# The gated attention of a recurrent layer dealt out with the experts' work, its last block in a place of its own, and six row products moved from VectorE to GpSimd

## The chip, the cores and the metric

The kernel runs on one core of a Trainium2 chip. The metric is the device time of one execution in microseconds (us). Engines are written as in the profile: PE is TensorE (PEld its weight loads), DVE is VectorE, ACT is ScalarE, POOL is GpSimd, SP is SyncE, which here only issues DMAs. Each engine takes its instructions strictly in order, from a queue of its own.

## The reference

The input x has 8 sequences of 512 steps and 256 features; all is in 32 bits. Two branches read the same normalised rows, and their product is added to x:

```python
xn = layernorm(x)
# recurrent attention, 16 heads of 16, for each sequence and step:
S = S * exp(gk); S = S + k * (a @ S + v); o = q @ S
attn = layernorm(o * sigmoid(xn @ Wog1 @ Wog2)) @ Wo
# mixture of experts, the best 2 of 8 for each of the 4096 rows:
moe = layernorm(sum over the two of w_e * (gelu(xn @ W1[e] + b1[e]) @ W2[e] + b2[e]))
out = x + attn * silu(moe)
```

## The kernel before

The 512 steps are cut into 8 blocks of 64 (all 8 sequences together: 512 rows to a block), and a block into chunks of 16 or 8 steps, alternately by block, 48 chunks in all. The recurrence walks the chunks in order; its arithmetic within a chunk (`fine`, `solve`) is done on DVE ahead of the walk. A chunk of the walk is `by_state` (products with the state S on PE, L901, and the decayed copy of S on ACT, L911), `add_v` (DVE, L932, and the rows it stores to `ro`, L943 and L948), `by_keys` (PE, L966) and `renew` (DVE, L978). Two blocks later the block's output is made: `load_output` (R from `ro`, 16 to a half, L1009 and L1012) and `output` (DVE, L1029 and L1038, stored as `o`, L1042).

The experts' branch is a list of 39 tiles of up to 256 sorted rows (`experts`). A tile loads 1 MB for each of its two weights (`w`, L1069 and L1071, on SP, two places in turn), gathers rows (L1081, POOL), multiplies (`ph`, L1125), takes gelu (`h`, L1133), multiplies again (`py`, L1150), scales by the gate's weight (`y`, L1158) and scatters with addition into `y_dram` (L1102, POOL). It also copies x to out piece by piece (L1139, SP).

`attend(s)` is the rest of the attention branch for block s. It loads the state's part (`by_state`, L1196, 8 DMAs) and the block's own part (`o_f`, L1204, 2 DMAs), then the inner gate rows (`og`, L1210, 2 DMAs), all on SP; it adds (DVE, L1213), makes the outer gate (PE `p`, L1220, written "p2" in the code and the text; sigmoid `sg` on ACT, L1224), multiplies (DVE, L1227), normalises (`moments` on DVE, L1171 and L1172; `deviation`, with the square root on ACT at L1177 and L1179, L1180 on DVE; `normed` on ACT, L1184), transposes (`pz`, L1241; `zT`, L1242) and multiplies by Wo (`po`, L1248). For blocks 0 to 5 the result is copied (ACT, L1265) and stored to `att_d` (POOL, L1269). Blocks 6 and 7 (`LATE`) multiply the gated sums `g` by `po` straight out of PSUM (DVE, L1256) and store them into `out` with addition (POOL, L1259). The tiles o, t and og1 have one place each, and the next block's loads wait until the last reader is done.

After the experts, `fetch_sums` loads the eight blocks of sums (`g`, L1275, POOL), and `finish(s)` normalises them, applies gamma and beta (DVE, L1291 and L1293) and silu (ACT, L1294); for blocks 0 to 5 it loads the stored attention (`att_f`, three places, L1302, POOL), multiplies (DVE, L1304) and stores into `out` with addition (two DMAs, L1307, POOL).

The order around the change: three queues of generators. `inner` holds the work ahead of the walk and the outputs, `beside` the experts and later the `finish` of all blocks (four lanes), `between` the attention. `both(share, other)` spends `share` on `inner`, a share on `between` and `other` on `beside`, in eight rounds; a generator yields the cost of what it has issued, or WAIT. After the 48th chunk the three are spent at 3.0 each until they are empty. The order in which a framework's scheduler then hands the instructions to each engine follows these turns.

Of the kernel before, what the change touches and what calls it, by code (L numbers as in the profile page):

```python
# [9 lines left out]
F32 = mybir.dt.float32  # L10
I32 = mybir.dt.int32
AF = mybir.ActivationFunctionType
ALU = mybir.AluOpType
# [4 lines left out]
P = 128  # L18
NB = 64
# [11 lines left out]
def recurrent_attn_moe_kernel(  # L31
# [23 lines left out]
    nc = tc.nc  # L55
    B, T, D = x.shape
    H = Wgamma.shape[1]
    HD = D // H
    E, _, DFF = W1.shape
    KD = D // P  # L60
    NF = DFF // P
    NTB = T // NB
    NP = B * NB // P
# [15 lines left out]
    def bank(name):  # L79
        return ps_p.tile([P, 512], F32, tag="ps", name=name)  # L80
# [30 lines left out]
    kqd_d, g_d, og_d, f1_d, v_d, fq_d, pc_d, kt_d, ro_d, o_d, att_d = ([] for _ in range(11))  # L111
# [28 lines left out]
    sp = ctx.enter_context(tc.tile_pool(name="inner", bufs=2))  # L140
    vz = []
    for i in range(2):
        t = sp.tile([P, GC, 2 * D], F32, name=f"vz{i}", bufs=1)
# [9 lines left out]
    made, now = {}, {}  # L153
# [192 lines left out]
    for q in range(4):  # L346
        for n in range(4):
            lo = 32 * q + E * n
# [292 lines left out]
    def behind(ins, first):  # L641

        tc.add_manual_dep(
            ins.ins,
            first.ins.name,
            mybir.DependencyInfo(mybir.DependencyClass.NoSync, mybir.DependencyReason.DATA),
            reason="what it waits for has that long",
        )
# [199 lines left out]
    solved = []  # L848


    cp, pending = [], []
# [209 lines left out]
    LATE = (NTB - 2, NTB - 1)  # L1061
    WAIT = "nothing to do yet"
# [106 lines left out]
    def moments(pool, t, i, mv):  # L1169
        st = pool.tile([P, 6], F32, name="st_f", bufs=4)  # L1170
        nc.vector.bn_stats(st, t)  # L1171
        nc.vector.bn_aggr(mv[:, i], st)  # L1172
# [10 lines left out]
    def normed(t, i, r):  # L1183
        nc.scalar.activation(  # L1184
            t, t, AF.Identity, bias=r[:, 1, i : i + 1], scale=r[:, 0, i : i + 1]
        )

    def attend(s):
        while (s, NB // CS[s] // 2 if s == NTB - 1 else 0) not in loaded:
            yield WAIT  # L1190
        pool = cp[0]
        o = pool.tile([P, NP, D], F32, name="o_f", bufs=1)
        t = pool.tile([P, NP, D], F32, tag="t_f", name="by_state", bufs=1)
        for bb in range(2):
            for q in range(4):
                nc.sync.dma_start(  # L1196
                    t[bb * NB : (bb + 1) * NB, q],
                    ro_d[s][q, CS[s] :, :, bb * D : (bb + 1) * D].rearrange("i c d -> c i d"),
                )
            yield 1.0  # L1200
        while s not in written:
            yield WAIT
        for bb in range(2):
            nc.sync.dma_start(  # L1204
                o[bb * NB : (bb + 1) * NB],
                o_d[s].rearrange("t (c bb) d -> bb t c d", bb=2)[bb],
            )
        og1 = pool.tile([32 + HD, B * NB], F32, name="og1", bufs=1)
        for lo in (0, 32):
            nc.sync.dma_start(og1[lo : lo + HD], og_d[s])  # L1210
        for _ in range(1 if s in LATE else SLACK):
            yield 1.0
        behind(nc.vector.tensor_tensor(o, o, t, ALU.add), now["work"])  # L1213
        yield 1.2
        sg = pool.tile([P, NP, D], F32, tag="t_f", name="sg", bufs=1)
        p2s = [bank("p2").rearrange("p (n d) -> p n d", n=2) for _ in range(NP // 2)]
        for k in range(2):
            for i, p2 in enumerate(p2s):
                at, n = slice(32 * i, 32 * i + HD), 2 * i + k
                nc.tensor.matmul(  # L1220
                    p2[:, k], og1[at, n * P : (n + 1) * P], wog2_sb[at], start=True, stop=True
                )
        for i, p2 in enumerate(p2s):
            nc.scalar.activation(sg[:, 2 * i : 2 * i + 2], p2, AF.Sigmoid)  # L1224
        yield 1.0
        yield 1.0
        nc.vector.tensor_tensor(o, o, sg, ALU.mult)  # L1227
        mv = pool.tile([P, NP, 2], F32, name="mv_f", bufs=1)
        for i in range(NP):
            moments(pool, o[:, i], i, mv)  # L1230
        yield 3.0
        r = yield from deviation(pool, mv)
        for i in range(NP):
            normed(o[:, i], i, r)
        yield 1.0
        zT = pool.tile([P, NP, KD, P], F32, tag="t_f", name="zT", bufs=1)
        for i in range(0, NP, 2):
            pz = bank("pz").rearrange("p (n j t) -> p n j t", n=2, j=KD)
            for k in range(2):
                for j in range(KD):  # L1240
                    nc.tensor.transpose(pz[:, k, j], o[:, i + k, j * P : (j + 1) * P], ident)  # L1241
            nc.scalar.copy(zT[:, i : i + 2], pz)  # L1242
            yield 1.0
        for i in range(0, NP, 2):
            po = bank("po").rearrange("p (n d) -> p n d", n=2)
            for k in range(2):
                for j in range(KD):
                    nc.tensor.matmul(  # L1248
                        po[:, k], zT[:, i + k, j], wo_sb[:, j],
                        start=(j == 0), stop=(j == KD - 1),  # L1250
                    )
            if s in LATE:
                while s not in gated:
                    yield WAIT
                g = gated[s][:, i : i + 2]
                nc.vector.tensor_tensor(g, g, po, ALU.mult)  # L1256
                yield 2.0
                for bb in range(2):
                    nc.gpsimd.dma_start(  # L1259
                        rows_of(out, s, bb)[:, i : i + 2],  # L1260
                        g[bb * NB : (bb + 1) * NB],
                        accum_op=ALU.add,
                    )
                continue
            nc.scalar.copy(o[:, i : i + 2], po)  # L1265
            yield 2.0
        if s in LATE:
            return
        nc.gpsimd.dma_start(att_d[s].rearrange("n p d -> p n d"), o)  # L1269
        attended.append(s)  # L1270
# [10 lines left out]
    def finish(fp, s, g):  # L1281
        mv = fp.tile([P, NP, 2], F32, name="mv_g", bufs=4)
        for i in range(NP):
            moments(fp, g[:, i], i, mv)
        yield 2.5
        r = yield from deviation(fp, mv)
        for i in range(NP):
            normed(g[:, i], i, r)
        yield 1.0
        wide = [P, NP, D]  # L1290
        nc.vector.tensor_tensor(g, g, now["gam"].unsqueeze(1).to_broadcast(wide), ALU.mult)  # L1291
        yield 1.2
        nc.vector.tensor_tensor(g, g, now["bet"].unsqueeze(1).to_broadcast(wide), ALU.add)  # L1293
        nc.scalar.activation(g, g, AF.Silu)  # L1294
        yield 1.2
        if s in LATE:
            gated[s] = g
            return
        while s not in attended:
            yield WAIT  # L1300
        att = fp.tile([P, NP, D], F32, name="att_f", bufs=3)
        nc.gpsimd.dma_start(att, att_d[s].rearrange("n p d -> p n d"))  # L1302
        yield 1.0
        nc.vector.tensor_tensor(g, g, att, ALU.mult)  # L1304
        yield 1.2
        for bb in range(2):
            nc.gpsimd.dma_start(  # L1307
                rows_of(out, s, bb), g[bb * NB : (bb + 1) * NB], accum_op=ALU.add
            )
# [41 lines left out]
    def both(share, other):  # L1351
        for _ in range(8):
            inner.spend(share / 8)
            between.spend(share / 16)
            beside.spend(other / 8)

    late = ExitStack()
# [8 lines left out]
    def everything_else():  # L1366

        for s in range(2, NTB):
            yield from project(s, xT_all[:, s])
        while not cp:  # L1370
            yield WAIT
        projecting.close()
        prologue.close()
        with tc.tile_pool(name="moe", bufs=2, side="right") as mp:
            yield from experts(mp)
        fp = late.enter_context(tc.tile_pool(name="fin", bufs=2, side="right"))
        for name, ap in (("gam", gamma), ("bet", beta)):
            now[name] = fp.tile([P, D], F32, name=f"{name}_sb", bufs=1)
            nc.sync.dma_start(now[name], ap.partition_broadcast(P))
        sums = [fetch_sums(fp, s) for s in range(NTB)]  # L1380
        yield 1.0
        for s in range(NTB):
            beside.queue.append(finish(fp, s, sums[s]))

    inner, beside, between = Work(1), Work(4), Work(1)
    beside.queue += [sorting(), everything_else()]

    def with_output(s):
# [8 lines left out]
        )  # L1397

    def attention():
        for s in range(NTB):  # L1400
            yield from attend(s)

    def recurrence():
# [59 lines left out]
    fetch(0)  # L1463
    turn_keys(0)
    inner.queue.append(recurrence())
    between.queue.append(attention())
    cost = fine_cost(0)
    for _ in range(4):
        both(cost / 4, EARLY / 4)
# [8 lines left out]
    n = NB // CS[NTB - 1]  # L1478
# [39 lines left out]
```

## Time and profile before

| | us |
|---|---|
| median of 3 runs | 1146.72 |
| lowest and highest | 1145.83, 1148.68 |
| the profiled execution's own time | 1136.74 |
| its span in the trace | 1135.0 |
| PE, DVE, ACT, POOL busy | 884.4, 882.3, 657.4, 372.7 |
| mean granted TensorE clock | 0.875 |
| by-state products of chunk 48 begin | 986.6 |
| last scaling of an expert's rows (L1158) begins | 1056.8 |
| first moments of the sums (L1171) begin | 1070.4 |
| last store into out is issued | 1129.7 |

Times within the profile count from the start of its span. A line number is one of the kernel before. A group of instructions is read as line, engine, operation, output<-inputs, shape, count, then busy time and mean of one, then the engine's idle time just before them and what ended it.

### The profile page before, as it was taken

The page shows a single profiled execution, that of the slowest core. Times are in us where ns is not written, and L with a number is a line of the kernel's source. Part 1 is how long each engine was busy: PE and PEld are TensorE (multiplying, and loading weights), DVE is VectorE, ACT ScalarE, POOL GpSimd, SP SyncE. Part 2 cuts the span into 40 slices and gives each one's busy share as a digit, 9 for nine tenths or more (in the row PEclk, how much of TensorE's full clock was granted, in tenths as well). Part 3 has the DMA queues.
Part 4 walks back from the last instruction along what each step waited for, and adds up shares of the span by engine and source line. Part 5 has one row for each costly group of instructions (what it writes and reads, how often), then busy time and mean ns, then how long its engine had stood idle before and what let it go on. Part 6 is the DMA issues. An engine that isn't in the chain of part 4 may idle for free. (4 is left out here: it accounts for less than half of the span.)

```text
span 1135.0 us, 24853 instructions
## 1 busy us (share of the span) xinstructions
PE 884.4 (78%) x9448; PEld 685.0 (60%) x9448; DVE 882.3 (78%) x1769; ACT 657.4 (58%) x1559; POOL 372.7 (33%) x312
## 2 busy tenths in 40 slices
PE   4979988636889989797969976989799599867402
PEld 2534645325777778576858754877677488756301
DVE  6479998957999998699999679999698183321494
ACT  2664537447455759745695665556955446535485
POOL 3300000052237633245324331367433243320334
PEclk9986998758899999889989996999899799887756
DMA  9666688598577999969789896878969979983786
GB/s 224 181 175 193 157 229 147 125 272 247 122 200 228 126 262 238 190 194 217 221 172 204 191 252 157 212 248 229 143 190 252 157 193 221 209 218 104 225 189 106
DMA packets 393254, 221.86 MB, mean 195 GB/s; under 512 B 280912, under 2 KB 362704, under 8 KB 392112
## 3 DMA queue, kind: packets, MB, share of 16 engines
q1 hardware_dynamic: 363248, 172.17, 61.4%
q0 software_dynamic: 25280, 43.93, 18.4%
q10 hardware_dynamic: 4608, 4.20, 1.5%
q8 instruction: 74, 1.21, 0.5%
q14 instruction: 44, 0.36, 0.1%
HBM read 152.07 MB, written 72.35 MB: 198 GB/s over the span
## 5 line engine op out<-in xcount | busy, mean ns | idle before, releaser
L1125 PE MATMUL ph<-xT_s,w 128*128 128x256 f32 (+1 forms) x1248 | 289.1, 389 | 13.8 <-DMA w<-in_L_ffn_W_dram 7.2
L1150 PE MATMUL py<-w,h 128*128 128x256 f32 x1136 | 270.0, 394 | 22.4 <-ACT h L1133 18.1
L1125 PEld LDWEIGHTS ph<-xT_s,w 128*128 128x128 f32 x1248 | 235.0, 207 | 50.4 <-issue 9.7
L1102 POOL DMA_INDIRECT y_dram<-y,target x71 | 159.3, 2244 | 316.9 <-ACT y L1158 154.2
L1150 PEld LDWEIGHTS py<-w,h 128*128 128x128 f32 x1136 | 218.5, 197 | 56.3 <-ACT h L1133 20.7
L911 ACT ACTIVATE sdec<-S,PcF 128x64 f32<-128x64 f32 x752 | 189.4, 341 | 91.4 <-DVE S L978 87.8
L1133 ACT ACTIVATE h<-ph,bias 128x256 f32<-128x256 f32 (+1 forms) x312 | 121.7, 453 | 97.8 <-PE ph L1125 97.5
L1081 POOL DMA_INDIRECT xs<-xn_dram,source x71 | 113.8, 1602 | 138.8 <-PE pt L1094 111.7
L978 DVE SCALAR_TENSOR_TENSOR S<-PC,heads,sdec 128x256 f32<-128x256 f32 x188 | 78.8, 473 | 51.9 <-PE PC L966 47.5
L1158 ACT ACTIVATE y<-py,weight 128x256 f32<-128x256 f32 x71 | 33.3, 469 | 87.5 <-PE py L1150 87.4
L901 PE MATMUL PC<-S,FA 64*16 64x64 f32 (+1 forms) x3072 | 44.3, 232 | 43.2 <-DVE S L978 43.0
L966 PE MATMUL PC<-RO,KT 8*64 8x64 f32 (+1 forms) x3008 | 49.4, 246 | 34.4 <-DVE RO L932 24.7
L966 PEld LDWEIGHTS PC<-RO,KT 8*64 8x64 f32 (+1 forms) x3008 | 41.5, 143 | 53.9 <-DVE RO L932 31.5
L811 DVE TENSOR_TENSOR scratch_a<-Z,A 128x1020 f32<-128x1020 f32 (+21 forms) x88 | 66.5, 756 | 5.3 <-ACT fq L775 4.7
L901 PEld LDWEIGHTS PC<-S,FA 64*16 64x16 f32 (+1 forms) x3072 | 34.7, 100 | 59.5 <-DVE S L978 49.9
L736 DVE TENSOR_TENSOR scratch_q<-Z,X 128x64 f32<-128x64 f32 (+11 forms) x96 | 69.6, 724 | 0.0
L749 DVE TENSOR_REDUCE Z<-scratch_q 128x4 f32<-128x64 f32 (+11 forms) x96 | 69.1, 720 | 0.0
L869 POOL MEMSET vz<- 128x1024 f32 x8 | 9.5, 1188 | 180.0 <-DVE RO L932 180.0
L819 DVE TENSOR_TENSOR Z<-Z,scratch_a 128x1020 f32<-128x1020 f32 (+21 forms) x88 | 66.4, 755 | 0.5
L753 DVE TENSOR_TENSOR Z<-Z,X 128x64 f32<-128x64 f32 (+10 forms) x88 | 59.7, 678 | 0.0
L736 DVE TENSOR_TENSOR scratch_a<-Z,X 128x64 f32<-128x64 f32 (+10 forms) x88 | 59.6, 678 | 0.0
L1241 PE MATMUL pz<-ident,o_f 128*128 128x128 f32 x64 | 12.6, 334 | 60.2 <-ACT o_f L1184 60.1
(227 smaller groups left out, 1383.3 us busy)
## 6 DMA issues: line engine op xcount, KB each, us to landing
w<-in_L_ffn_W_dram SPq DMA_DIRECT2D x78, 1024.0 KB
kqd<-st_p SPq DMA_DIRECT2D x48, 256.0 KB
raw<-kqd SPq DMA_DIRECT2D x8, 1536.0 KB
fq<-fq SPq DMA_DIRECT2D x8, 1024.0 KB
xn_dram<-xn SPq DMA_DIRECT2D x8, 512.0 KB
v<-st_p ACTq DMA_DIRECT2D x32, 128.0 KB
y_dram<-st_b SPq DMA_DIRECT2D x16, 256.0 KB
out_dram<-in_L_attn_x_dram SPq DMA_DIRECT2D x16, 256.0 KB
```

The lines of the kernel that those rows point to most:

```text
L736: nc.vector.tensor_tensor(pr, Z[:, :, :upto, C:], step[:, m, i].unsqueeze(2).to_broadcast([P, n, upto, HD]), ALU.mult,)
L749: now["work"] = nc.vector.tensor_reduce(to, pr, AX.X, ALU.add)
L811: nc.vector.tensor_tensor(pr, Z[:, :, l, l:].unsqueeze(2).to_broadcast([P, n, l, w]), A[:, :, l, :l].unsqueeze(3).to_broadcast([P, n, l, w ...
L901: nc.tensor.matmul(p1[32 * q : 32 * q + 2 * C, b, m], FA[lo : lo + SB, 4 * q + m, c], S[lo : lo + SB, q, m], start=True, stop=True,)
L911: nc.scalar.activation(dec[:, n // 4, n % 4], S[:, n // 4, n % 4], AF.Copy, scale=PcF[:, n, c : c + 1])
L966: nc.tensor.matmul(p4[b * SB : (b + 1) * SB, q, m], KT[32 * q : 32 * q + C, lo : lo + SB], ro[32 * q : 32 * q + C, lo : lo + SB], start=Tr ...
L978: nc.vector.scalar_tensor_tensor(S.rearrange(flat)[:, :, at], p4.rearrange(flat)[:, :, at], heads[:, h : h + 1], now["dec"].rearrange(flat ...
L1081: nc.gpsimd.indirect_dma_start(out=xs[:, n], out_offset=None, in_=xn_dram[:, :], in_offset=bass.IndirectOffsetOnAxis(ap=source[:, r : r + ...
L1102: nc.gpsimd.indirect_dma_start(out=y_dram[:, :], out_offset=bass.IndirectOffsetOnAxis(ap=target[:, r : r + 1], axis=0), in_=y, in_offset=None,
L1125: nc.tensor.matmul(ph[:, k, :size], w1[:, j, (f + k) * P : (f + k + 1) * P], xT[:, j, :size], start=(j == 0), stop=(j == KD - 1),)
L1133: nc.scalar.activation(h[:, k, :size], ph[:, k, :size], AF.Gelu, bias=bias[:, t, f + k : f + k + 1])
L1150: nc.tensor.matmul(py, hs[f // 2][:, f % 2, n * P : (n + 1) * P], w2[:, f], start=(f == 0), stop=(f == NF - 1),)
```

## The change

There are four edits. In `attend`, o, t and og1 become parts of one tile with one place; t serves in turn as the state's part, the gate and the transposed rows. The place of the last block's tile is that of another pool, under the tag "X", which the keys of the recurrence used before. The loads of `og` are issued first, before the block has been waited for in `loaded`. The scaled moments `mv_f` get the pool's two places. Blocks 6 and 7 stop before their transposes until the experts' last tile has been issued (`now["experts"]`).

`between` has two lanes, one for the attentions of blocks 0 to 6 and one for that of block 7, and is spent by the experts' share (0.04 of `other`) where it was spent by the recurrence's (1/16 of `share`). In `finish`, the product of the gated sums with the stored attention is issued on GpSimd, which then stores it.

```diff
     def attend(s):
+        while s not in solved or not cp:
+            yield WAIT
+        pool = cp[0]
+
+        W = NP * D
+        place, tag = (sp, "X") if s == NTB - 1 else (pool, "attn")
+        mine = place.tile([P, 2 * W + B * NB], F32, tag=tag, name="attn", bufs=1)
+        o, t = (mine[:, i * W : (i + 1) * W].rearrange("p (n d) -> p n d", d=D) for i in range(2))
+        og1 = mine[: 32 + HD, 2 * W :]
+        for lo in (0, 32):
+            nc.sync.dma_start(og1[lo : lo + HD], og_d[s])
         while (s, NB // CS[s] // 2 if s == NTB - 1 else 0) not in loaded:
             yield WAIT
-        pool = cp[0]
-        o = pool.tile([P, NP, D], F32, name="o_f", bufs=1)
-        t = pool.tile([P, NP, D], F32, tag="t_f", name="by_state", bufs=1)
...
-        og1 = pool.tile([32 + HD, B * NB], F32, name="og1", bufs=1)
-        for lo in (0, 32):
-            nc.sync.dma_start(og1[lo : lo + HD], og_d[s])
...
-        sg = pool.tile([P, NP, D], F32, tag="t_f", name="sg", bufs=1)
+        sg = t
...
-        mv = pool.tile([P, NP, 2], F32, name="mv_f", bufs=1)
+        mv = pool.tile([P, NP, 2], F32, name="mv_f")
...
-        zT = pool.tile([P, NP, KD, P], F32, tag="t_f", name="zT", bufs=1)
+        while s in LATE and "experts" not in now:
+            yield WAIT
+        zT = t.rearrange("p n (j t) -> p n j t", j=KD)
...
-        nc.vector.tensor_tensor(g, g, att, ALU.mult)
+        nc.gpsimd.tensor_tensor(g, g, att, ALU.mult)
...
-            between.spend(share / 16)
+            between.spend(0.04 * other)
...
             yield from experts(mp)
+        now["experts"] = True
...
-    inner, beside, between = Work(1), Work(4), Work(1)
+    inner, beside, between = Work(1), Work(4), Work(2)
...
     def attention():
-        for s in range(NTB):
+        for s in range(NTB - 1):
             yield from attend(s)
...
-    between.queue.append(attention())
+    between.queue += [attention(), attend(NTB - 1)]
```

## The prediction

> **What bounds the kernel now.** I read the page first: no engine is busy throughout, so the question is which stage the change touches.
>
> ```profile
> PE 884.4 (78%) x9448; PEld 685.0 (60%) x9448; DVE 882.3 (78%) x1769; ACT 657.4 (58%) x1559; POOL 372.7 (33%) x312
> ```
>
> The stretches of the last 155 us come next (columns: stretch and its length; busy time and instruction count of PE, PEld, DVE, ACT, POOL; granted clock, DMA share, GB/s).
>
> ```profile
> 980.00:1010.00 30.00, 28.75 (x234) 26.92 (x235) 7.10 (x20) 11.37 (x33) 6.13 (x7) 0.89 0.99 244
> 1010.00:1028.00 18.00, 2.77 (x14) 2.15 (x12) 6.27 (x27) 0.96 (x2) 3.49 (x1) 0.61 0.82 222
> 1028.00:1057.00 29.00, 25.26 (x133) 22.12 (x130) 3.32 (x11) 16.28 (x34) 2.40 (x2) 0.83 0.32 102
> 1057.00:1070.00 13.00, 0.00 (x0) 0.00 (x0) 4.21 (x10) 4.21 (x6) 7.55 (x9) 0.69 0.67 172
> 1070.00:1099.00 29.00, 7.45 (x32) 5.32 (x32) 27.43 (x90) 20.42 (x37) 9.65 (x13) 0.62 0.86 239
> 1099.00:1130.00 31.00, 6.43 (x24) 4.69 (x24) 19.19 (x31) 21.94 (x34) 15.54 (x16) 0.61 0.82 134
> ```
>
> Three things are to be seen. PE does 2.77 us of work in the 18 us of 1010–1028, with two tiles of the experts still to do. From 1057 to 1070 nothing much runs: the last scatter lands and the sums come back. Then DVE is nearly full (27.43 of 29) until 1099, POOL is not. The waits of 1000–1135 say who is late (engine, line, releaser: us in total, times, longest).
>
> ```profile
> ...
> DVE o_f L1213 <- DMA og<-og: 36.5, 2, 25.3
> ...
> POOL att_f L1302 <- DVE g L1304: 17.8, 1, 17.8
> ACT L1224 <- DVE o_f L1213: 15.9, 1, 15.9
> ...
> PE p L1220 <- DMA og<-og: 15.2, 1, 15.2
> ...
> POOL out_dram L1307 <- DVE g L1304: 9.5, 2, 8.5
> ```
>
> PE's 15.2 us is attention 5's p2 product, with tiles 37 and 38 queued behind it. SP's timeline gives the reason (start, length, engine, line, operation, count):
>
> ```profile
> 993.33 13.65 SPq L1012 DMA_DIRECT2D R<-ro  x16
> ...
> 1009.23 0.73 SPq L1196 DMA_DIRECT2D by_state<-ro  x1
> 1014.75 1.29 SPq L1042 DMA_DIRECT2D o<-O  x2
> 1016.09 5.41 SPq L1196 DMA_DIRECT2D by_state<-ro  x7
> 1021.61 1.21 SPq L1204 DMA_DIRECT2D o_f<-o  x2
> 1022.87 1.06 SPq L1210 DMA_DIRECT2D og<-og  x2
> 1024.98 0.41 SPq L1069 DMA_DIRECT2D w<-in_L_ffn_W_dram  x1
> ```
>
> Attention 5's og is issued last, behind 16 issues for R, and tile 37's weights stand behind it. Attentions 6 and 7 share its o and t places, so they come after the experts; 7's add starts at 1098.9, its po ends at 1126, the last store is issued by 1129.7 and the span ends 5.3 later.
>
> The profiled execution took 1136.74 (span 1135.0 and 1.7 around it), 9.98 under the median of 1146.72. I sum differences within it and take them off the median.
>
> **1. Attentions 0 to 5 earlier.** Work taken from `between` at 0.04 of the experts' share instead of 1/16 of the recurrence's moves attention 4's add from after the 42nd of the 48 chunks to after the 37th, and attention 5's from after chunk 47 to after chunk 42. The experts' tiles stay within one of where they were at each chunk. DVE pays 1.2 + 1.2 + 4 × (0.40 + 0.17) = 4.7 us per attention; attention 4's falls at 820–860 (DVE 37.7 of 40 busy), but DVE then idles 15.7 us at 860–900 for PE's L966, so I cost it nothing; without that idle it would be 4.7. On PE attention 5 brings p2 1.1, pz 1.05 and po 3.6 into the run-up to chunk 48, less attention 4's p2 (1.1): near +5, of which PE's idle (15.5 of 20 busy at 960–980) hides some; I take +3.
>
> SP counts more. Before tile 30's weights it now also issues attention 5's loads and og of 7 (14 issues, at 0.6 each some 8 us), and before tile 34's weights og of 6 and eight by_state loads (1.0 + 5.05 = 6). The first lag reaches tile 33 as some 7, the second adds 6: tile 34's weights are issued near 989 instead of 976, and since PE had 2–3 us in hand its second product ends near 1003 instead of 992.3. The second half of R stands behind them on SP: 1003 instead of 993.3, block 7's output ends at 1025 instead of 1014.9, and attention 7's loads, add, sigmoid and square root follow at 1033 to 1039. This part alone is a loss of 10, and all of it has cover in what part 2 frees.
>
> The early chunks: x's raw load for block 2 goes ahead of the first weights (POOL and DVE stalled 9.3 us near 288 there; 0 to −5), while each og now waits for the place that the preceding attention's store leaves, with SP's queue behind it (0 to +5 over three attentions). I let these cancel and keep ±5.
>
> **2. The hole of 1010–1028.** Attention 5's p2 is done by then, so the wait of 15.2 is gone. What is late next is tile 37's weights behind R (issued 1022.5 instead of 1025), and tile 38's, 1032. Tile 38's first product runs at 1038–1042, its gelus on ACT stand among 7's sigmoid and square root, each with a table load of 1.28 before and after: 1042 + 2.6 + 3.6 for the second product, so the last y scaling comes near 1048.5 instead of 1056.8: **−8.3**. Before, PE spent 25.3 us from 1028 to that scaling on the same two tiles; attention 5's products in it (5) and p2 of 6 are what falls away, so this is not a free shift of 15. The bounds are −15 (hole closed, nothing late) and +2 (ACT's chain of 7 holds tile 38).
>
> **3. The tail.** Let S be the start of the sums' moments, 13.6 after the last scaling (1056.8 to 1070.4 before; the scatter's landing and eight loads are unchanged). Before, the last issue ended at S+59.3. Now only pz (4.2 for both), po (8.9) and four 0.68 products of 6 and 7 remain, against the 25.3 that DVE waited for og. DVE's list shrinks to 32 × 0.40 + 32 × 0.16 + 16 × 1.22 + 2.7, some 40 us, and ends by S+40. ACT's is 16.1 + 8.0 + tables, some 32.
>
> So POOL becomes the end. Its order is: six products with their att_f loads, 12 stores, and the eight stores of 6 and 7, the last four at the very end. The first product needs the first silu, S+17.1 before (1087.5). From there: three more att_f loads (0.8 each, 2.4), 20 stores at 1.03 (four took 4.12), 20.6, six products of p, and the waits for an att_f that has only just been issued (landing 4 to 10 us after issue, some behind stores and products: 5.6). No row shows a GpSimd product of two inputs. The nearest are these (busy, mean ns):
>
> ```profile
> L869 POOL MEMSET vz<- 128x1024 f32 x8 | 9.5, 1188 | 180.0 <-DVE RO L932 180.0
> ...
> masks.py:199 POOL TENSOR_SCALAR_AFFINE_SELECT ident<-ident 128x128 f32<-128x128 f32 x1 | 0.3, 283 | 0.0
> ```
>
> The memset of 128x128 took 0.20, that of 1024 0.95 to 1.19: about 0.83 ns an element for writing. The select, one read and one write, is 0.28 for 128, which rises by 0.6 ns an element if 0.2 of it is the write. Two reads: 0.83 + 2 × 0.6 = 2.0, so p is near 2.2. Ends: 1.2 (a memset, or DVE's own 1.22) and 4.4 (double). With 2.2 the sum is 17.1 + 2.4 + 20.6 + 13.2 + 5.6 = S+58.9, against S+59.3: **−0.4**. Each further us of p costs 6. Had the products stayed on DVE, DVE's 40 + 7 would still end before POOL's 46, so this part of the change gives little and can cost.
>
> Here a rule speaks against the change. The rows: DVE's L1291 and L1293, two inputs each at 1.22, run between S+12 and S+36, just when POOL would multiply, and the memsets that gave 0.95 to 1.19 only write. The Trainium skill ("SBUF — State Buffer", Who interferes with whom) says that DVE and GpSimd share a port pair under an exclusive lock, which a two-input DVE operation takes. By that page I estimate one 1.22 wait for one to two of the products, or +1.2 to +2.4, and the sum would be about 1140. No row of before shows such a pair.
>
> **Sum.** −8.3 − 0.4 ± 5, near −9: 1146.7 − 9 = 1138.
>
> **Rivals.** *Slower: products on GpSimd.* POOL is in-order, so each product holds its stores, and p decides alone: at 4.4 it costs 6 × 2.2 = 13.2 more, 1138 + 13 = 1151; from p = 3.7 on (9 / 6 above 2.2) nothing is gained, and from 4.3 it is slower than can be explained by scatter. For it: no two-input row, and DVE busy beside it; against it: the select's 283 ns. *No change: attention 7's chain takes the hole's place.* Its sigmoid and square root stand in ACT's order among tile 38's gelus, and both wait for R by way of SP. If block 7's output ends 5 us later than I think, the last scaling is at 1055 and the tail gives 0.4: 1145. For it: p2 of 7 sits ready on PE and holds two of four banks from tile 36 on. *Better:* the weights are not late (SP had gaps at 960 and 985), the last scaling comes at 1043 and p is 1.2: −14 − 6, about 1128.
>
> **How the numbers follow.** The forecast's band of 1131 to 1143 gets 0.40, the better case 0.14, no change 0.13, and the slower one 0.33 since it has two bounds that I cannot see (p, and the SP waits of part 1). A measurement of this kernel can tell about 0.3%, 3.4 us. Range: 1127 to 1155, which leaves out a little on each side.
>
> **What would show it.** Right: no DVE or PE wait for og after chunk 48; the last L1158 some 8 us nearer to the start of the tail; POOL last with DVE done 15 us sooner; six products on POOL near 2.2. Wrong: a mean of over 3.7 for them; POOL idle for att_f of over 10; ACT's 7 chain ahead of the last gelus and a last scaling after 1053; chunk 48 later than 990 by more than 5.

## The result: slower by 1.5%

The changed kernel took 1164.62 us (median of four runs, 1160.77 to 1168.15) against 1147.70 of the kernel before in runs beside it; the ratio is 1.0153, interval 1.012 to 1.0187. Run again later it was 1.0154 (1.0114 to 1.0195). The forecast was 1138, with a range that ended at 1155.

The medians lie 17 us apart, the profiled executions 31.4 (spans 1166.4 and 1135.0): before's stands ten under its median and the changed kernel's 3.5 over its own. A second profile of the changed kernel has a span of 1157.1; between the two, chunk 48 differs by 7.7 us, the stage after it by 2.2 and the tail by 0.6 (the stages are those of the table below). A smaller difference between two profiles in one of these is not read as an effect.

The stretches after chunk 48, as shown of before (same columns):

```profile
1010.00:1028.00 18.00, 11.31 (x169) 9.56 (x169) 8.82 (x20) 1.88 (x6) 2.26 (x5) 0.62 0.76 223
1028.00:1057.00 29.00, 22.57 (x127) 18.72 (x126) 11.32 (x42) 14.81 (x34) 4.66 (x3) 0.94 0.79 186
1057.00:1070.00 13.00, 8.18 (x44) 7.69 (x45) 0.00 (x0) 4.05 (x10) 0.05 (x1) 0.74 1.10 268
1070.00:1099.00 29.00, 19.63 (x104) 16.41 (x102) 4.93 (x14) 12.34 (x24) 11.02 (x12) 0.93 0.46 140
1099.00:1130.00 31.00, 0.00 (x0) 0.00 (x0) 30.96 (x89) 23.98 (x44) 14.87 (x11) 0.50 0.49 147
1130.00:1166.00 36.00, 0.00 (x0) 0.00 (x0) 9.33 (x12) 7.20 (x9) 24.30 (x22) 0.50 0.90 138
```

At 1010–1028 the recurrence's walk is still going (169 matmuls, where before had the 18 us hole), and the experts' tiles fill PE up to 1085. The last 36 us belong to POOL: DVE has 9 us of work in them, POOL 24. The waits after 1030 have lost the two long ones for `og`; DVE and PE wait for block 7's rows and for weights instead (engine, line, releaser: total, times, longest):

```profile
POOL y_dram L1102 <- ACT y L1158: 56.1, 5, 16.1
...
POOL g L1311 <- ACT g L1301: 15.2, 1, 15.2
DVE attn L1218 <- DMA attn<-o: 14.1, 1, 14.1
...
PE ph L1125 <- DMA w<-in_L_ffn_W_dram: 5.3, 1, 5.3
```

Three milestones divide every trace into stages: the add of chunk 48 (the last L932), the last scaling (L1158), and the first moments of the sums (L1171), from which the tail runs to the end of the last issue for `out`.

| kernel | ratio to before | chunk 48 | to the last scaling | tail |
|---|---|---|---|---|
| before | 1 | 987.6 | 69.2 | 59.4 |
| changed | 1.0153 | 1019.9 | 65.2 | 62.2 |
| changed, second profile | 1.0154 | 1012.2 | 63.0 | 62.8 |
| changed, products on VectorE (a2) | 1.0100 | 1011.6 | 62.7 | 55.2 |
| a2, block 7 behind 6 (c2) | 1.0030 | 1006.5 | 54.0 | 61.6 |
| a2, block 7 held back (h1) | 0.9978 | 1002.4 | 53.0 | 53.9 |
| before, new pace (b2) | 1.0043 | 1009.0 | 56.2 | 60.0 |
| before, products on GpSimd (b1) | 1.0035 | 988.6 | 68.6 | 64.5 |

Between the last scaling and the first moments lie 13 to 14 us in each.

### The profile page after: what moved, and what is told of

It reads as the page before. It is cut to its first block, busy times and chain, and to the rows that moved or that the text cites. A ratio compares the mean times of both kernels' runs of the same rounds, so it can differ in the third digit from the quotient of the medians.

```text
span 1166.4 us, 24862 instructions
## 1 busy us (share of the span) xinstructions
PE 892.9 (77%) x9448; PEld 686.5 (59%) x9448; DVE 882.5 (76%) x1763; ACT 668.2 (57%) x1566; POOL 395.2 (34%) x318
## 3 DMA queue, kind: packets, MB, share of 16 engines
q1 hardware_dynamic: 363248, 172.17, 59.4%
## 5 line engine op out<-in xcount | busy, mean ns | idle before, releaser
L1125 PE MATMUL ph<-xT_s,w 128*128 128x256 f32 (+1 forms) x1248 | 289.5, 391 | 16.3 <-DMA w<-in_L_ffn_W_dram 14.7
L1125 PEld LDWEIGHTS ph<-xT_s,w 128*128 128x128 f32 x1248 | 236.1, 208 | 54.4 <-issue 17.9
L1081 POOL DMA_INDIRECT xs<-xn_dram,source x71 | 119.6, 1685 | 172.5 <-PE pt L1094 136.2
L901 PE MATMUL PC<-S,FA 64*16 64x64 f32 (+1 forms) x3072 | 50.2, 234 | 55.1 <-DVE S L978 42.7
L932 DVE TENSOR_TENSOR RO<-PC,vz 128x512 f32<-128x512 f32 x48 | 33.0, 688 | 70.4 <-PE PC L901 58.2
L966 PE MATMUL PC<-RO,KT 8*64 8x64 f32 (+1 forms) x3008 | 54.2, 248 | 41.2 <-DVE RO L932 33.9
L1158 ACT ACTIVATE y<-py,weight 128x256 f32<-128x256 f32 x71 | 33.3, 468 | 86.0 <-PE py L1150 85.8
L966 PEld LDWEIGHTS PC<-RO,KT 8*64 8x64 f32 (+1 forms) x3008 | 44.2, 144 | 63.3 <-DVE RO L932 40.8
L811 DVE TENSOR_TENSOR scratch_a<-Z,A 128x1020 f32<-128x1020 f32 (+21 forms) x88 | 67.1, 762 | 3.9 <-ACT fq L775 3.4
L869 POOL MEMSET vz<- 128x1024 f32 x8 | 8.2, 1028 | 177.8 <-DVE RO L932 176.1
L819 DVE TENSOR_TENSOR Z<-Z,scratch_a 128x1020 f32<-128x1020 f32 (+21 forms) x88 | 67.0, 762 | 0.6
```

What stands on the lines that cost most here:

```text
L811: nc.vector.tensor_tensor(pr, Z[:, :, l, l:].unsqueeze(2).to_broadcast([P, n, l, w]), A[:, :, l, :l].unsqueeze(3).to_broadcast([P, n, l, w ...
L901: nc.tensor.matmul(p1[32 * q : 32 * q + 2 * C, b, m], FA[lo : lo + SB, 4 * q + m, c], S[lo : lo + SB, q, m], start=True, stop=True,)
L966: nc.tensor.matmul(p4[b * SB : (b + 1) * SB, q, m], KT[32 * q : 32 * q + C, lo : lo + SB], ro[32 * q : 32 * q + C, lo : lo + SB], start=Tr ...
L1081: nc.gpsimd.indirect_dma_start(out=xs[:, n], out_offset=None, in_=xn_dram[:, :], in_offset=bass.IndirectOffsetOnAxis(ap=source[:, r : r + ...
L1125: nc.tensor.matmul(ph[:, k, :size], w1[:, j, (f + k) * P : (f + k + 1) * P], xT[:, j, :size], start=(j == 0), stop=(j == KD - 1),)
```

## The experiments

Ratios are to the kernel before in the same job, with 95% intervals. The times in the expectations count on 1147.7 us for the kernel before; from job to job its median was 1138.2 to 1147.8 (1138.67 for a1, a2, a3 and b1), so ratios are compared. The changed kernel's whole 1.5% is taken apart first, then the pace, then other versions.

### The products on GpSimd

```diff
-        nc.gpsimd.tensor_tensor(g, g, att, ALU.mult)     # a2, in the changed kernel
+        nc.vector.tensor_tensor(g, g, att, ALU.mult)
-        nc.vector.tensor_tensor(g, g, att, ALU.mult)     # b1, in the kernel before
+        nc.gpsimd.tensor_tensor(g, g, att, ALU.mult)
```

a2: 

> The changed kernel with the six products on VectorE again. By the tail's own sum (POOL's chain from the first silu without 6 products of 2.8, DVE with 7.2 more and done before it): the tail from the first moments to the last issue shortens from 62 to 48 or 52 us, the whole by 10 to 14: 1150 to 1155. If the stores and the landing of att_f set POOL's pace and not its products: 1161 to 1165. Theory S and theory P both leave chunk 48 as late as it is, near 1015.

b1: 

> The kernel before with nothing but the six products on GpSimd. There POOL had 17.8 + 9.5 us of idle in the tail and attention 7 ended last; a product of 2.8 in place of 1.22, six times, is +9.6 on POOL, and -7.2 on DVE, of which attention 7 can gain some. Theory G (the products are the loss): 1153 to 1160. The others: 1144 to 1150.

Measured: a2 1.0100 (1.0058 to 1.0141), b1 1.0035 (1.0012 to 1.0057). The tail is 7.0 us shorter with the products back on VectorE (62.2 to 55.2) and 5.1 longer with them on GpSimd in the kernel before (59.4 to 64.5): less than was expected of either, and so were the ratios (a2 at 1150 to 1155 us would be 1.002 to 1.006, b1 at 1153 to 1160 would be 1.005 to 1.011). The products themselves, in the changed kernel and in b1 (line, engine, operation, shape, count, then busy, mean ns, and idle before):

```profile
L1311 POOL TENSOR_TENSOR g<-g,att_f 128x1024 f32<-128x1024 f32 x6 | 16.7, 2789 | 21.9 <-ACT g L1301 15.2 <-DMA att_f<-att 6.7
```

```profile
L1304 POOL TENSOR_TENSOR g<-g,att_f 128x1024 f32<-128x1024 f32 x6 | 17.8, 2965 | 23.0 <-ACT g L1294 15.1 <-DMA att_f<-att 7.9
```

Their line alone, by durations (ns, shortest/median/longest):

```profile
L1311 POOL TENSOR_TENSOR g<-g,att_f x6: 2335/2350/3840, 1115.9 to 1149.2; 128x1024 f32<-128x1024 f32 x6
```

Four of the six take 2.3 to 2.35. The first and the sixth, and what DVE did near them (start, length, engine, line, operation, count; the last row is DVE's last instruction):

```profile
1115.87 3.84 POOL L1311 TENSOR_TENSOR g<-g,att_f 128x1024 f32<-128x1024 f32 x1 [15.18 <-ACT g L1301]
1126.33 2.35 POOL L1311 TENSOR_TENSOR g<-g,att_f 128x1024 f32<-128x1024 f32 x1 [0.18 <-DMA att_f<-att]
1147.93 2.47 POOL L1314 DMA_DIRECT2D out_dram<-g  x2
1149.24 3.53 POOL L1311 TENSOR_TENSOR g<-g,att_f 128x1024 f32<-128x1024 f32 x1
```

```profile
1115.14 2.35 DVE L1300 TENSOR_TENSOR g<-g,bet_sb 128x1024 f32<-128x1024 f32 x2
1126.36 3.39 DVE L1300 TENSOR_TENSOR g<-g,bet_sb 128x1024 f32<-128x1024 f32 x1
1138.66 1.29 DVE L1263 TENSOR_TENSOR g<-g,po 128x512 f32<-128x512 f32 x2 [0.58 <-ACT g L1301]
```

The first product takes 1.5 longer while an addition of beta is under way on DVE, until 1117.49. Where the product is first, at 1126.33, it is DVE's addition that takes 3.39; the eight average 1.49 against 1.22 in a2. So both engines pay, by turns. This agrees with the Trainium skill's rule ("SBUF — State Buffer", Who interferes with whom) for a DVE operation with two inputs and a GpSimd operation that reads. The sixth product is another matter: it begins nine us after DVE's end, while the issue of two stores ahead of it still runs (until 1150.40), and why it takes 1.2 longer is not shown. The second profile has the same two long products. Together the six took 2.7 more than six times 2.34: 1.5 beside DVE, for which I had estimated 1.2 to 2.4, and 1.2 in the sixth.

### The common place

```diff
-        sg = t
+        sg = t if s == NTB - 1 else pool.tile(...tag="t_f", name="sg"...)   # a3; o, by_state, og1, zT alike
```

> The changed kernel with o, t and og of blocks 0 to 6 in three tiles again, loaded in the old order (og last); block 7 keeps its own place, and pace, wait and products stay changed. Theory S: the 20 us in which SP waited for a store to land are gone; chunk 48 begins 8 to 15 us earlier and the time is 1150 to 1157. Theory P: 1161 to 1166.

Measured 1.0180 (1.0145 to 1.0216), with chunk 48 at 1011.6. In the changed kernel SP did wait:

```profile
SPq L1199 <- DMA att<-attn: 20.2, 2, 11.0
```

In a3 this wait is gone and nothing is faster. The forecast's bound of 5 us for these waits was a quarter of what SP waited, and it did not matter here. a3's 1.0180 would be 1168 us at 1147.7, a little above Theory P's 1161 to 1166 too.

### Block 7's lane, its place, and the wait for the experts

```diff
-        while s in LATE and "experts" not in now:        # c1: the wait before the transposes left out
-            yield WAIT
+        place, tag = (pool, "attn")                       # c2: block 7 in the common place and lane
+        while s not in solved or not cp or (s == NTB - 1 and "experts" not in now):   # h1
```

All four have the products on VectorE; c3 has the old pace as well.

c1: 

> The changed kernel with the products on VectorE and without the wait of blocks 6 and 7 for the experts' last tile: their transposes and Wo products go among the last tiles. If the wait only sorts work that has slack on both sides: 1.008 to 1.012 of before, like the kernel with the products back alone (1.010). If PE and ACT are what the last tiles need: 1.012 to 1.02. If the tail ends on blocks 6 and 7: below 1.006.

c2: 

> The changed kernel with the products on VectorE and block 7's attention behind block 6's in one lane and the one common place. Theory: what the own place gives is attention 7's loads and gate before the tail; without it they come after block 6's last reader, so the tail ends on block 7 as in the kernel before: 3 to 12 us more than with the products back alone, 1.013 to 1.02 of before. Rival: SP's and ACT's queues are freed of block 7 in the last tiles, which come 5 us earlier: 1.004 to 1.009.

c3: 

> The changed kernel with products and pace as before: left are the one tile for o, t and og, block 7's own place and lane, and the wait of 6 and 7. Theory O (block 7's attention, free to run in a lane of its own among the last tiles, holds ACT, SP and PSUM banks there): from chunk 48 to the last scaling 68 to 80 us, as in the changed kernel with only the pace back (72.5), the tail 3 to 8 shorter than with the products on GpSimd, 1.008 to 1.014 of before. If the products were what made that kernel slow (1.020): 0.998 to 1.004.

h1: 

> The changed kernel with the products on VectorE, and block 7's attention still in its own place and lane, but started only when the experts' last tile has been issued. Theory O: from chunk 48 to the last scaling 52 to 58 us (54.0 with block 7 in order behind 6, 62.7 with it free), the tail up to the last issue 55 to 59 (55.2 and 61.6), together 0.994 to 1.000 of before. If the 8.7 us between those two kernels are scatter, or come from the place itself: 60 or more, 1.004 to 1.012.

Measured: c1 1.0224 (1.0183 to 1.0266), c2 1.0030 (1.0008 to 1.0053), c3 1.0115 (1.0085 to 1.0146), h1 0.9978 (0.9958 to 0.9999). From chunk 48 to the last scaling: c1 80.4, a2 62.7, c2 54.0, h1 53.0, c3 73.6. Holding block 7 back while it keeps its own place takes the changed kernel's order from 1.010 to 0.998, as Theory O expected; c3 too lies where it had it. Without the wait for the experts the same order is 1.2% slower still (c1, above all that I had expected), so this part of the change pays. My expectation for c2, a tail on block 7, was right for the tail (61.6) and wrong for the sum, since the stage ahead gave back more (8.7).

How a free block 7 costs the last tiles is in SP's timeline. a2 (start, length, engine, line, operation, count):

```profile
1028.65 11.33 SPq L1012 DMA_DIRECT2D R<-ro  x16
1040.02 5.09 SPq L1204 DMA_DIRECT2D attn<-ro  x8
1046.47 0.41 SPq L1069 DMA_DIRECT2D w<-in_L_ffn_W_dram  x1
1047.57 3.86 SPq L1042 DMA_DIRECT2D o<-O  x2
1051.68 1.56 SPq L1071 DMA_DIRECT2D w<-in_L_ffn_W_dram  x1
1055.23 1.21 SPq L1212 DMA_DIRECT2D attn<-o  x2
1057.28 0.40 SPq L1069 DMA_DIRECT2D w<-in_L_ffn_W_dram  x1
```

h1:

```profile
1019.22 11.22 SPq L1012 DMA_DIRECT2D R<-ro  x16
1031.31 0.40 SPq L1069 DMA_DIRECT2D w<-in_L_ffn_W_dram  x1
1031.95 0.40 SPq L1071 DMA_DIRECT2D w<-in_L_ffn_W_dram  x1
1037.97 1.34 SPq L1042 DMA_DIRECT2D o<-O  x2
1040.99 0.38 SPq L1069 DMA_DIRECT2D w<-in_L_ffn_W_dram  x1
```

Counted from the start of R, tile 37's first weights are issued at +17.8 in a2 and +12.1 in h1: block 7's eight by_state loads stand between. PE waits for them (a2, tile 37's first product; idle before in brackets):

```profile
1051.87 6.18 PE L1125 MATMUL ph<-xT_s,w 128*128 128x128 f32 x32 [5.05 <-DMA w<-in_L_ffn_W_dram]
```

The same for h1, tiles 37 and 38:

```profile
1036.40 3.81 PE L1125 MATMUL ph<-xT_s,w 128*128 128x128 f32 x32 [1.36 <-DMA w<-in_L_ffn_W_dram]
1046.48 5.44 PE L1125 MATMUL ph<-xT_s,w 128*128 128x128 f32 x32 [2.60 <-DMA w<-in_L_ffn_W_dram]
```

In h1 tile 37's product starts 17.2 after R, in a2 23.2. It also takes 3.81 against 6.18; the granted clock is 1.00 in h1's and 0.60 in a2's (stretches as above, a2 first):

```profile
1051.87:1058.05 6.18, 6.18 (x33) 6.11 (x34) 0.00 (x0) 1.87 (x6) 0.00 (x0) 0.60 1.13 243
1036.40:1040.21 3.81, 3.81 (x34) 3.81 (x35) 1.86 (x13) 1.88 (x6) 2.15 (x1) 1.00 0.97 243
```

From the end of that product to the last scaling a2 takes 16.3 and h1 15.2. In a2 block 7's sigmoid and square root stand there among tile 38's gelus, with four table loads of 1.28; in h1 PE waits 2.60 for tile 38's weights and then takes 5.44. a2's ACT:

```profile
1059.05 1.28 ACT L1229 ACT_TABLE_LOAD   x1
1062.16 1.08 ACT L1229 ACTIVATE attn<-p 128x512 f32<-128x512 f32 x2 [1.83 <-DVE attn L1218]
...
1064.58 1.28 ACT L1133 ACT_TABLE_LOAD   x1 [0.97 <-PE ph L1125]
...
1066.78 1.28 ACT L1177 ACT_TABLE_LOAD   x1
...
1068.39 1.28 ACT L1133 ACT_TABLE_LOAD   x1
```

So of the 9.7 us by which this stage differs, 6.0 are there by the start of tile 37's first product, through SP, 2.4 come in that product and 1.1 after it, the balance of a2's table loads and h1's wait for weights. h1 takes loads, banks and chain of block 7 out together; the division is read from these two traces.

### The pace

```diff
-            between.spend(0.04 * other)                  # a1, in the changed kernel
+            between.spend(share / 16)
-            between.spend(share / 16)                    # b2, in the kernel before
+            between.spend(0.04 * other)
+            between.spend(share / 14)                    # e1; e2: share / 18
```

a1: 

> The changed kernel with the attentions paid for as before (1/16 of the recurrence's share); all other edits stay. Theory P (the pace moves attentions into a stage without room, and what stands behind them is late): most of the 17 us goes, 1147 to 1153, and chunk 48 begins within 8 us of the kernel before's 987.6. Theory S (SP's queue waits for the one place that o, t and og share, until the preceding attention's store has landed): the place stays, so 1159 to 1166. Theory G (GpSimd's products): 1163 to 1166.

b2: 

> The kernel before with nothing but the attentions' new pace (0.04 of the experts' share); one lane, old places, products on VectorE. Theory W (each attention that is done before chunk 48 makes the recurrence's walk some 9 us longer, since its instructions stand in every engine's queue between two steps of the walk, and after chunk 48 some of that comes back): chunk 48 begins 15 to 22 us later than in the kernel before, what follows is 15 to 25 shorter, the sum 0.990 to 1.004 of before. Theory N (the pace is harmless, as the forecast had it: +3 at chunk 48): chunk 48 within 8 us, the sum 0.985 to 0.995. If the 24 us come from the two lanes or the own place, chunk 48 is within 8 us here too.

e1: 

> The kernel before with 1/14 of the recurrence's share for the attentions in place of 1/16: attention 4 is done by the 40th chunk instead of after the 48th, attentions 5 to 7 stay behind chunk 47. Half the dose of the new pace. If each attention moved ahead of chunk 48 costs its PE and waits there (12 us of PE for two of them and as much again in waits): chunk 48 begins 8 to 14 us later, and what follows is 5 to 12 shorter, 0.998 to 1.006 of before. If it is the arrangement as such that costs (any shift disturbs chunks that fitted): chunk 48 later by more than 15. If the pace is harmless in this dose: within 4.

e2: 

> The kernel before with 1/18 of the recurrence's share for the attentions in place of 1/16: attention 4's second part and all of 5 to 7 stay behind chunk 48, as before, but each attention meets other chunks and tiles. If the number of attentions ahead of chunk 48 is what counts: chunk 48 within 5 us of the kernel before (988 to 999 in profiles of the same order), 0.996 to 1.004. If the arrangement counts (which chunk and which tile an attention meets): later by 10 to 25, as with 1/14, 1.005 to 1.03.

Measured: a1 1.0201 (1.0171 to 1.0230), b2 1.0043 (1.0022 to 1.0065), e1 1.0340 (1.0316 to 1.0364), e2 1.0227 (1.0196 to 1.0257). Chunk 48 stands at 994.7, 1009.0, 1019.1 and 988.8; from there to the last scaling it takes 72.5, 56.2, 89.6 and 83.0. So the new pace alone makes chunk 48 later (21 us here) and gives 13 back in the stage after it, close to Theory W. a1 is the same trade from the other side: chunk 48 is 25 earlier than in the changed kernel, the stage after it 7 longer and the tail 9 (71.3), so that with the old pace the changed kernel is, if anything, slower (1.0201 against 1.0153), which none of a1's three theories had. Both neighbours of the old pace are far worse than either: e1 is 31 later at chunk 48 and 20 longer in the stage after it, e2 level at chunk 48 and 14 longer after it. The number of attentions ahead of chunk 48 does not order these runs. That the arrangement does, which chunk and which tile an attention meets, is what is left and not shown.

Three kernels that leave work out asked what makes chunk 48 late.

```diff
-            nc.scalar.activation(sg[...], p2, AF.Sigmoid)                # e3 (new pace) and e4 (old)
+            nc.scalar.activation(sg[...], p2, AF.Gelu)
-        r = yield from deviation(pool, mv)
+        nc.vector.reciprocal(r[:, 0], mv[:, :, 1])                       # no square root
+        if s < 4: ...store o, return                                     # d1, after the add (old pace)
```

e3: 

> The kernel before with the new pace, and the attentions' sigmoid replaced by gelu and their square root left out (the reciprocal is taken of the variance), so that they ask for no table that the experts' gelus do not have. Order as in the kernel with the pace alone. Theory T (ACT's table loads, five more of them among the gelus before chunk 48 and each 1.28 us, hold the walk's scaled copies and PE's second products): chunk 48 within 8 us of the same cut of the kernel before, and the ratio between the two below 1.000. Theory P (PE's products themselves): still 15 to 22 later, ratio 1.002 to 1.007.

e4: 

> The kernel before with the same cut (gelu for the attentions' sigmoid, no square root): the base of the comparison, and the price of the tables there. Some 15 to 20 table loads fewer before chunk 48, 20 to 26 us of ACT. Theory T: chunk 48 begins 5 to 15 us earlier, 0.985 to 0.995 of before. Theory P: within 4 us, 0.995 to 1.000.

d1: 

> The kernel before, in which blocks 0 to 3 leave out everything of the attention between the add and the store (gate, norm, transposes, Wo), with the same loads and the same cost in the queues: four attentions' worth of instructions out of the walk. It prices an attention in the walk. Theory W: chunk 48 begins 28 to 40 us earlier, 7 to 10 for each. Theory N (they fit beside the walk): 0 to 10 earlier in all.

Measured: e3 1.0040 (1.0014 to 1.0067), e4 0.9926 (0.9900 to 0.9952), d1 1.0239 (1.0215 to 1.0263), with chunk 48 at 1010.8, 998.8 and 1003.6. Without the tables and square roots the kernel before is 0.7% faster, though its chunk 48 comes 11 later, and the one with the new pace keeps its time and its chunk 48. Between e4 and e3 the pace makes chunk 48 12.0 later and costs 1.1%, more than the 0.4% with the tables in place: they are not the cause. Neither theory has these numbers within its bounds. And d1, with four attentions' work gone, is slower, 16 us later at chunk 48 and with 89.8 us from there to the last scaling: a kernel with less work but another arrangement of its queues. Both of my expectations for d1 were wrong.

What can be said of the walk is in its stretches. Before, chunks 19–22 and 43–46, and b2 the same chunks (columns as above):

```profile
512.05:559.43 47.38, 40.82 (x542) 33.44 (x540) 47.38 (x63) 29.56 (x80) 19.78 (x13) 0.93 0.85 223
905.35:959.15 53.80, 53.80 (x619) 45.99 (x620) 31.91 (x84) 29.47 (x86) 24.72 (x12) 0.97 0.79 215
```

```profile
516.35:572.09 55.74, 51.14 (x589) 43.00 (x590) 54.43 (x71) 34.57 (x98) 25.21 (x14) 0.94 0.57 163
920.41:983.50 63.09, 60.19 (x643) 50.42 (x643) 32.34 (x89) 37.83 (x106) 31.05 (x12) 0.96 0.81 209
```

Before, the first is full on DVE and the second on PE; in b2 they are 8.4 and 9.3 longer. What the attentions bring explains a part only. In the second, po and pz bring PE 5.0, and PE idles 2.9. In the first the attention's share of DVE is no larger than before (3.8 for 4.6): the 7.1 that DVE has more are the recurrence's own L811 and L819 (`solve`) and the outputs' L1029 and L1038, which fell into other chunks before. The lag also comes and goes: b2 is 6 behind at chunk 38, 21 at 40, 15 at 43 and 21 at 48. From chunk 7 to chunk 48 the attentions of b2 bring 12.9 us more to PE (po 7.5, pz 3.5, p2 1.9), 5.0 to DVE and 19 to ACT. PE and DVE make 17.9, against 19 between the mean positions of chunk 48 (993 in eight profiles with the pace of 1/16 and nothing of the work or only the tables left out, 987.6 to 998.8; 1012 in nine with the new pace, 1002 to 1028). That the two agree is no proof: in d1 less work brought chunk 48 no earlier, and why is open.

### Attentions 5 to 7 after the experts

```diff
+        while s >= NTB - 3 and "experts" not in now:     # f1, in the kernel before; 5 joins LATE
+            yield WAIT
+        between.queue += [attend(s) for s in LATE]       # g4: in three lanes, places "X" and in the sums' pool
+        if s == NTB - 2: ...14 turns first               # g5: og loaded first, 6 last
```

f1: 

> The kernel before with attention 5 treated like 6 and 7, and its loads held until the experts' last tile has been issued: PE's wait of 15 us for og at 1011 to 1026, with tiles 37 and 38 behind it, goes without anything being moved ahead of chunk 48. The last scaling comes 10 to 14 us earlier; the tail gets 7 us more of DVE and 6 of PE and ends on three attentions in one place after another (15 each before): 0.992 to 1.000 of before. Rival: the tail is a chain of loads for the shared places, and a third attention in it costs more than the hole: 1.003 to 1.01.

g4: 

> A version meant to beat both: the kernel before with old pace and products on VectorE, attentions 5, 6 and 7 all started after the experts' last tile, in three places (the common one, one in the pool of the sums, block 7's as in the changed kernel) and three lanes, all three multiplied straight into the sums. The run-up as before; chunk 48 to the last scaling 43 us, as with three late attentions in one place (42.9, whose tail was 85.6); the tail is DVE's list, 40 + 6 products of 1.2 + three attentions of 4.7, some 61, and ends at 65 to 74: 0.980 to 0.992 of before. Rival: the loads of all three are queued on SP and land late, or ACT's tables bind: tail over 80, 0.995 to 1.003.

g5: 

> As with the three places for attentions 5 to 7, but og is loaded first, 5 and 7 go ahead, and 6 starts its loads 14 turns later, so that 5 and 7 no longer wait on SP behind 6's place (there the first add stood at 1067, 37 us after the last scaling). The two adds come near 1040, before the sums; from the sums' moments to the last issue 60 to 70 us instead of 80.7: 0.980 to 0.990 of before. Rival: the tail is set by ACT's order (tables, normed rows) and not by the loads: 75 or more, 0.993 to 0.998.

Measured: f1 0.9991 (0.9967 to 1.0015), g4 0.9957 (0.9931 to 0.9983), g5 0.9964 (0.9938 to 0.9990). With no attention among the last tiles chunk 48 to the last scaling takes 42.9, 42.0 and 42.0, against 69.2 before: this stage's 27 us were real. But the tail takes 85.6, 80.7 and 80.8, and hands most of it back. In g4 I blamed SP's loads; g5 moved them and the tail stayed. Its rival was ACT's order, which no run tested alone; the number of table loads does not explain it, since the same tail has 7 of them in g4 and 14 in g5. What sets this tail is open; g4 and g5 came out at their rivals. g4 and g5 are faster than before by 0.4%, h1 by 0.2% with an interval that ends at 0.9999, and all three are faster than the changed kernel.

The changed kernel once more: 

> The changed kernel itself, unaltered, once more: a second profile and a ratio from the same chip as the version above. 1.011 to 1.019 of before; chunk 48 between 1005 and 1022, 62 to 68 us to the last scaling, tail 60 to 64. If its first profile had been an outlier: chunk 48 below 1000.

 Measured 1.0154, chunk 48 at 1012.2, 63.0 and 62.8 for the two stages: as expected.

## Why the prediction was wrong, step by step

The step that failed is the first term, +3 at chunk 48; the start of R behind it and the length of a product were smaller misses. The forecast was +3 at chunk 48, −11.3 in the stage after it and −0.4 in the tail, near −9; by the second profile they are +24.6, −6.2 and +3.4.

**Part 1, +3 on PE at chunk 48: mis-sized, the largest term.** Chunk 48 came at 1020 and 1012, 25 to 32 after before's profile. By the means over all profiles of either pace, 993 and 1012, the pace's own share is 19. I counted attention 5's 5.8, less 1.1, and left out that attention 4's pz and po stood behind chunk 48 as well (995.9 to 1003.9) and move ahead of it (875 to 894 in b2). PE got the pz and po of two attentions and p2 of one (12.9). DVE's idle time of 15.7 us at 860–900, my cover for attention 4, was a wait for PE, and it is there that these products came to run. Why 12.9 on PE and 5.0 on DVE come with 19 at chunk 48 is open. ACT's eight further table loads (10.3 of the 19 on ACT) were not priced; e3 says that they did not matter.

**Part 1, the SP waits of 0 to +5:** 20.2 by the trace, without effect by a3.

**Part 2, −8.3 at the last scaling (−11.3 from chunk 48): right from R on, with R's start 5 us too early.** The wait for og is gone and the stage became shorter, by 4 to 6 instead of 11. I had the second half of R at 1003, 12.4 after chunk 48. In the changed kernel it begins 17.1 and 17.2 after it, behind the weights of tile 36 (SP, second profile; the last row is tile 37's weights):

```profile
1021.09 6.41 SPq L1069 DMA_DIRECT2D w<-in_L_ffn_W_dram  x1
1029.43 11.33 SPq L1012 DMA_DIRECT2D R<-ro  x16
1047.24 0.41 SPq L1069 DMA_DIRECT2D w<-in_L_ffn_W_dram  x1
```

From R's start the forecast has tile 37's weights at +19.5 and the last scaling at +45.5; the second profile has +17.8 and +45.8, the first +17.8 and +48.1. So attention 7's chain among the last tiles was priced nearly right, and what came is the condition of the second rival, block 7's output 5 us late. What I did not see is that this chain is a cost that can be avoided: with block 7 held back, h1 needs 36.2 from R to the last scaling, where a2 needs 45.7, and its stage is 16 shorter than before's, more than I forecast.

One reading of before was a tile off. The weights issued at 1024.98 are the last of 39, those of tile 38; tile 37's were issued at 1008.07, behind R and ahead of og, and its product stood behind p2's wait alone (SP's timeline, then the summary of these issues: shortest, median and longest issue in ns, first and last start):

```profile
1008.07 0.41 SPq L1069 DMA_DIRECT2D w<-in_L_ffn_W_dram  x1
L1069 SPq DMA_DIRECT2D w<-in_L_ffn_W_dram x39: 375/407/3947, 237.2 to 1025.0; - x39
```

**Part 3, the tail at S+58.9: mechanism right, p too small.** POOL ended last, DVE at S+41.3 where I had S+40, and the last issue at 62.2 and 62.8. p was 2.79 for 2.2, which is 6 × 0.59 = 3.5 us. The bare product (2.34) was close to the estimate from the affine select; of the 0.45 above it, a little over half is the contention with DVE, which I had estimated and left out of the sum, and the rest the long sixth product. The sentence on products left on DVE was wrong by its own numbers: DVE's 40 + 7 ends after POOL's 46, and against that 47 the forecast had the move of the products as a loss of 12. a2's tail of 55.2 makes it 7.0.

**By ratios.** Against h1 the list is shorter: 1.2% for block 7's free lane (h1 to a2) and 0.5% for the products (a2 to the changed kernel, with intervals that overlap); all else in the change together is worth 0.2% of gain, since the stage after chunk 48 gives back what chunk 48 is late. The first rival, products at 4.4, named the right sign for a smaller reason.

## What to carry to other kernels

Work moved ahead into "idle" time must be priced on every engine in the stretch where it lands: DVE's idle time, taken for cover here, was a wait for PE, and part of the moved work was PE's. In front of a finish that waits for a few last tiles, see what stands on the DMA queue ahead of their weights and on ACT between their activations: holding the moved work back until the last tile had been issued was worth 1.2%, more than any other part. And a pace constant has a rough landscape: 1/14 and 1/18 cost 3.4% and 2.3% where 1/16 had been found, so a new pace is to be tried at several values before its idea is judged.

## What the runs showed that was not expected

- Leaving out four attentions' gate, norm and products made the kernel 2.4% slower: 16 us later at chunk 48 and 20 longer in the stage after it.
- Contention of DVE and GpSimd showed on both sides: a product of 2.34 took 3.84 beside an addition of DVE, and an addition of 1.22 took 3.39 beside a product.
- Without the attentions' table loads (1.28 us each) and square roots the kernel before was 0.7% faster, though ACT is busy only 58% of the span.
